# Four transformer-like layers on one NeuronCore: when a softmax loop sums its values, and what stands beside them

## The chip, the core and the metric

The kernel runs on one core of a Trainium2 chip. TensorE (PE) multiplies matrices, VectorE (DVE), ScalarE (ACT) and GpSimd (POOL) work on rows of 128 partitions, and SyncE (SP) issues most DMAs. The metric is the device time in microseconds from the first to the last instruction of one execution; the median of three executions is given, with the lowest and the highest.

## The reference, cut to what matters

`x` is 4 batches of 512 tokens with 288 features, all in fp32. Layer L0 rotates 64 of its directions per batch. L1, L2 and L3 are attention blocks with 16 heads of 18 features, each modulated by a condition; L1 and L2 end in an MLP of width 1152, L3 in a mixture of four experts, two per token. L2 also normalizes each query and each key head. The loop that changes computes this, for each of 12 attentions (3 layers by 4 batches):

```python
scores = jnp.einsum('blhd,bmhd->bhlm', q * scale, k)
attn = jax.nn.softmax(scores, axis=-1)
o = jnp.einsum('bhlm,bmhd->blhd', attn, v).reshape(b, l, c)
```

## The kernel before, in words

`attend(n, ...)` is called for attention n = 0 to 11, layer n // 4 and batch n % 4. Its 16 heads are taken in four groups of four, G = 4n to 4n + 3, because a head has 18 features and so fits in a strip of 32 partitions. A group has eight steps, so `attend` has 32. A step does two things with the scores of four heads, and both write a PSUM tile of 128 by 1024 of the same ring of two (`pbig`):

- `maxima` works ten steps ahead (`LOOK = 10`). Two matmuls give scores `p_s` with queries down the partitions, and DVE's `tensor_reduce` takes their maxima into `M`.
- `weigh` works at the step itself. Two matmuls give scores `p_st` with keys down the partitions, and ACT's exponential turns them into `e`, a ring of six.

Each of these matmuls has 32 rows and uses one of PE's four strips of rows, so the four of a step lie side by side. Before `weigh` may start on a group, `take_maxima` transposes its maxima (`p_m`, four transposes) and DVE subtracts them from the queries in place (`Q`, in `store`).

`give_values` sums the values: for one tile of 128 keys, four matmuls with 128 rows and 32 columns each (`p_av`), one per head, lie side by side in four strips of columns. A tile of keys takes two steps of `weigh`, so `ready` gets an entry at each odd step. After a group's fourth tile, ACT copies `p_av` to `o`, and five DMAs take it to DRAM.

What else PE has to do stands in generators that `attend` draws from, the `fill`: `project` makes queries, keys and values of attention n + 1 (`p_qk`, `p_v`), `finish` the output projection of attention n - 1 (`p_o`), `layernorm` the transposed input (`p_t`) of the next projection and the next MLP, and L2's `project` also the variances of its heads (`p_var`). Each `yield` names the piece's cost in us. `attend` adds a share of the attention's total to `left` after each step and draws pieces until `left` is used up: 0.5 us more at odd steps and 0.5 less at even ones, since even steps also sum values. The second generator, `norms`, draws one small DVE piece per step: statistics and normalized rows (`s`, `mv`, `rstd`, `xn`) and the inverse sums (`oc`). After attention 1 to 8, `mlp` runs the MLP of attention n - 1 in one stretch (`p_h`, `p_y`), with one call of `give_values` in its first part.

288 features are 128 + 128 + 32. `project` therefore works in pairs of jobs: the two full matmuls of each job, and then the tails, two matmuls with 32 rows that lie side by side in two strips. They come wherever `left` happens to run out.

Engines execute in the order in which the program issues, so the order of the Python calls is the order on each queue. A matmul in fp32 is two passes in the profile.

Of the kernel before, what the change touches and what calls it, by code (L numbers as in the profile page):

```python
# [17 lines left out]
NT = 4  # L18
# [5 lines left out]
NG = 4  # L24
# [23 lines left out]
def cond_seq_kernel(ctx: ExitStack, tc: tile.TileContext, a: dict, out: bass.AP):  # L48
# [227 lines left out]
    gtab = rows.tile([6 * B, C], F32, name="gtab")  # L276
    btab = rows.tile([2, B, C], F32, name="btab")

    md = mods.tile([128, C], F32, name="md")
    nc.gpsimd.memset(md, 0.0)  # L280
    was = {}

# [14 lines left out]
    def modulations(ns):  # L297

        for n in ns:
            l, half = divmod(n, 2)  # L300
            if half == 0:
                mt = mts[l] = const.tile([128, 4, KW + 1, B], F32, name=f"modT{l}")
                nc.gpsimd.memset(mt, 0.0)
            gr = mods.tile([B, C], F32, tag="gr", name=f"gr{n}")
            p = pmm(f"p_mod{n}")
            for k in range(KC):
                for s in range(3):
                    matmul(p[s * 32:s * 32 + B, :C], scT[0:kk(k), k, :],
                           was[n][0:kk(k), k, s * C:(s + 1) * C], start=(k == 0), stop=(k == KC - 1))
                yield 0.5  # L310
            for s in range(2):
                q = (2 * half + s) * 32
                scalar.copy(md[q:q + B], p[s * 32:s * 32 + B, :C])
            scalar.copy(gr, p[64:64 + B, :C])
            dma(gtab[n * B:(n + 1) * B], gr)
            if half and l < 2:
                br = mods.tile([B, C], F32, tag="br", name=f"br{l}")
                load(br, row(a[("L1_cond_b_fc2", "L2_cond_b2")[l]]).to_broadcast([B, C]))
                nc.gpsimd.tensor_mul(br, br, gr)
                dma(btab[l], br)  # L320
            if n == 5:
                sr = mods.tile([B, C], F32, tag="br", name="sr")
                scalar.activation(sr, p[32:32 + B, :C], AF.Copy, bias=1.0)
                dma(mrow.rearrange("s b c -> (s b) c")[0:B], md[64:64 + B])
                dma(mrow.rearrange("s b c -> (s b) c")[B:2 * B], sr)
                dma(mrow.rearrange("s b c -> (s b) c")[2 * B:], gr)
            if n + 2 < 6:
                load_ada(n + 2)
            if half:
                pt = pmm(f"p_modT{l}")  # L330
                for k in range(KW + 1):
                    w = 128 if k < KW else TAIL
                    transpose(pt[:w, k * 128:(k + 1) * 128], md[:, k * 128:k * 128 + w], ident)
                    for i in range(1 if k < KW else STRIPS):
                        scalar.copy(mts[l][i * TAIL:i * TAIL + w, :, k, :],
                                    pt[:w, k * 128:(k + 1) * 128].rearrange("p (s r) -> p s r", r=32)[:, :, :B])
                for s in (1, 3):
                    nc.gpsimd.tensor_scalar_add(mts[l][:, s], mts[l][:, s], 1.0)
                modT.append(mts[l])
                yield 0.6  # L340
# [20 lines left out]
    with tc.tile_pool(name="l0", bufs=1) as l0, tc.tile_pool(name="l0w", bufs=2) as l0w, \  # L361
# [4 lines left out]

        zP = hT[1][:, 0:2, :]
        MT = hT[1][0:D, KW, 0:B * D]
        At = mods.tile([D, C], F32, name="At")
        X = l0.tile([D, 2 * D], F32, name="X")  # L370
        Wt = l0.tile([D, D], F32, name="Wt")
        pt = pmm("p_G")
# [638 lines left out]
    with tc.tile_pool(name="attn", bufs=2) as at:  # L1011
# [14 lines left out]

        def project(n, norm):

            l, b = divmod(n, B)
            wqk, wv = WA[l][:2]  # L1030
            h = hT[0]
# [4 lines left out]
            def qk_job(m):  # L1036
                w = min(QP, QK - m * QP)
                cols = slice(m * QP, m * QP + w)
                p = pmm(f"p_qk{n}_{m}")

                def evict():
                    bias = QB[l][0:w, m:m + 1]
                    t = at.tile([QP, T], F32, tag="stage", name=f"stage{n}_{m}", bufs=3)[0:w]
                    if l != 1:
                        scalar.activation(t, p[0:w], AF.Identity, bias=bias, scale=scol[0:w, m:m + 1])
                    else:
                        tmp = at.tile([128, 2, T], F32, tag="e", name=f"tmp{n}_{m}", bufs=6)
                        sq, rs = tmp[0:w, 0, :], tmp[0:w, 1, :]
                        scalar.activation(sq, p[0:w], AF.Square, bias=bias)
                        vector.tensor_scalar(t, p[0:w], bias, None, ALU.add)  # L1050
                        yield 0.0
                        pv = pmm(f"p_var{n}_{m}")
                        matmul(pv[0:w], varsel.rearrange("p h d -> p (h d)")[0:w, 0:w], sq, start=True, stop=True)
                        scalar.activation(rs, pv[0:w], AF.Ln, bias=eps5[0:w])
                        scalar.activation(rs, rs, AF.Exp, scale=-0.5)
                        yield 0.86
                        vector.scalar_tensor_tensor(t, t, gains[0][0:w, m:m + 1], rs, ALU.mult, ALU.mult)
                        nc.gpsimd.tensor_scalar(t, t, gains[1][0:w, m:m + 1], None, ALU.add)
                    dma(flat[cols], t)
                return p[0:w], 0.86, lambda k, r: (wqk[r, k, cols], h[r, k, :]), evict  # L1060
# [12 lines left out]
            for i in range(0, len(jobs), 2):  # L1073
                pair = []
                for job, arg in jobs[i:i + 2]:
                    p, cost, operands, evict = job(arg)
                    for k in range(KW):
                        matmul(p, *operands(k, slice(0, 128)), start=(k == 0), stop=False)
                        yield cost
                    pair.append((p, operands, evict))  # L1080
                for e in later:
                    yield from e
                for q, (p, operands, evict) in enumerate(pair):
                    matmul(p, *operands(KW, strip(q)), start=False, stop=True)

                later = [e for e in [evict() for p, operands, evict in pair] if next(e, None) is not None]
                yield 0.95
                if i <= NQ - 1 < i + 2:
                    for e in later:
                        yield from e  # L1090
                    later = []

                    src = qd.rearrange("(s g i) d t -> s i d g t", s=2, i=4)
                    for s, t in enumerate((Q[n % 2], K[n % 2])):
                        for q in range(4):
                            dma(t[q * HS:q * HS + HD], src[s, q])
                    for q in range(4):
                        dma(Q[n % 2][q * HS + HD:q * HS + VS], zero_row[q:q + 1].rearrange("a (g t) -> a g t", t=T))
                    there.add(n)
                    yield None  # L1100
# [88 lines left out]

        def attend(n, fill, total, norms):  # L1190

            left = 0.0
            for step in range(8 * NG):
                g, s = divmod(step, 8)
                G = NG * n + g
                ahead, mstep = divmod(8 * G + s + LOOK, 8)
                if ahead < NG * NB:
                    while ahead // NG not in there:
                        next(fill)
                    maxima(ahead, mstep)  # L1200
                E.append(weigh(G, s))
                if s == 8 - 2 and G + 1 < NG * NB:
                    take_maxima(G + 1)
                if s % 2 == 0:
                    give_values()
                left += total / (8 * NG) + (0.5 if s % 2 else -0.5)
                next(norms, None)
                while left > 0:
                    cost = next(fill, "end")
                    if cost == "end":  # L1210
                        break
                    left -= cost or 0.0
                if s % 2:
                    ready.append((G, s // 2))
            for _ in fill:
                pass
            for _ in norms:
                pass

        def give_values():  # L1220

            if not ready:
                return
            G, c = ready.pop()
            if c == 0:
                PO[0] = pacc(f"p_av{G}")
            sum_values(G, PO[0], c, E[:2])
            del E[:2]
            if c == NT - 1:
                t = at.tile([128, T], F32, tag="o", name=f"o{G}", bufs=3)  # L1230
                scalar.copy(t, PO[0])
                n, g = divmod(G, NG)
# [61 lines left out]
        for t in range(LOOK):  # L1294
# [1 line left out]
            if t == 8:  # L1296
                take_maxima(0)
            next(rest, None)
            next(new)
            if t == 5:  # L1300
                projection_bias(0)
        for n in range(NB):
# [49 lines left out]
            if 2 <= n < 2 + 2 * NE:  # L1352
                fill_table(n - 2)
            attend(n, itertools.chain(*fill), total, first_ready(side))
            if n == 2 or n == B + 2:
                projection_bias(l + 1)
                head_biases(l + 1)
# [156 lines left out]
```

## Time and profile before

| what | us |
|---|---|
| median of 3 runs (lowest to highest) | 2094.88 (2086.53 to 2099.71) |
| profiled execution | 2086.44 |
| its span | 2084.7 |
| PE busy in the span | 1901.0 |
| DVE busy | 928.8 |
| ACT busy | 781.3 |
| the twelve attentions, from first to last score step (213.7 to 1647.4), the eight MLPs in between included | 1433.7 |
| one MLP with the step before it, mostly | 39.9 |
| the experts and what follows | 437.3 |

An attention starts at its first `weigh`: attention 1 at 300.6, attention 4 at 699.7, attention 8 at 1240.0 and so on. In the timeline a row is a run of instructions of one kind on one engine, with its start, its length, its shape (rows x columns of the stationary operand, or output and input), and in brackets the idle time of the engine before it, with what ended it. Most rows have L60 as their line, that of the helper (`InOrder`) through which the kernel calls PE, DVE and ACT, so rows are told apart by their tiles. In a table of stretches each engine's busy us stand with the number of instructions, and PEclk is the share of PE's full clock that was granted.

### The profile page before, as it was taken

The page shows a single profiled execution, that of the slowest core. Times are in us where ns is not written, and L with a number is a line of the kernel's source. Part 1 is how long each engine was busy: PE and PEld are TensorE (multiplying, and loading weights), DVE is VectorE, ACT ScalarE, POOL GpSimd, SP SyncE. Part 2 cuts the span into 40 slices and gives each one's busy share as a digit, 9 for nine tenths or more (in the row PEclk, how much of TensorE's full clock was granted, in tenths as well). Part 3 has the DMA queues.
Part 4 walks back from the last instruction along what each step waited for, and adds up shares of the span by engine and source line. Part 5 has one row for each costly group of instructions (what it writes and reads, how often), then busy time and mean ns, then how long its engine had stood idle before and what let it go on. Part 6 is the DMA issues. An engine that isn't in the chain of part 4 may idle for free. (4 is left out here: it accounts for less than half of the span.)

```text
span 2084.7 us, 26249 instructions
## 1 busy us (share of the span) xinstructions
PE 1901.0 (91%) x10269; PEld 927.7 (44%) x10269; DVE 928.8 (45%) x1953; ACT 781.3 (37%) x1169; POOL 252.2 (12%) x362
## 2 busy tenths in 40 slices
PE   6769879999999999899999999998987899999997
PEld 4544223343523434234234343333322367777775
DVE  6764646346164362562634526355576334111111
ACT  5122454434254343443444434444444322212111
POOL 1000010001010020010100000000000212332322
PEclk9578999999999999999999999999999989999999
DMA  3212152031131221511203112061221445766663
GB/s 97 71 40 62 37 153 81 17 96 29 40 73 26 72 58 42 135 42 54 75 22 85 33 54 80 23 137 30 82 50 61 172 147 175 238 187 219 203 202 95
DMA packets 89420, 187.23 MB, mean 90 GB/s; under 512 B 25454, under 2 KB 50457, under 8 KB 86803
## 3 DMA queue, kind: packets, MB, share of 16 engines
q1 hardware_dynamic: 77462, 103.39, 18.8%
q0 software_dynamic: 11248, 79.79, 11.8%
q10 hardware_dynamic: 584, 2.36, 0.4%
q8 instruction: 81, 1.33, 0.3%
q14 instruction: 45, 0.36, 0.1%
HBM read 152.49 MB, written 55.45 MB: 100 GB/s over the span
## 5 line engine op out<-in xcount | busy, mean ns | idle before, releaser
L60 DVE TENSOR_REDUCE store<-p_s 128x2 f32<-128x1024 f32 x384 | 470.4, 1225 | 370.3 <-PE p_st L60 324.0
L60 ACT ACTIVATE e<-p_st 128x1024 f32<-128x1024 f32 x384 | 393.1, 1024 | 643.9 <-PE p_st L60 639.6
L60 PE MATMUL p_s<-store 32*128 32x512 f32 x1536 | 445.4, 652 | 83.0 <-DVE store L60 81.7
L60 PE MATMUL p_st<-store 32*128 32x512 f32 x1536 | 444.2, 655 | 0.9 <-DVE store L60 0.9
L60 PEld LDWEIGHTS p_s<-store 32*128 32x128 f32 x1536 | 120.6, 186 | 315.9 <-DVE store L60 230.1
L60 PE MATMUL p_av<-e,store 128*32 128x512 f32 x1536 | 212.5, 626 | 2.0 <-ACT e L60 2.0
L60 PE MATMUL p_he<-hTe,store 128*128 128x256 f32 (+1 forms) x1026 | 200.1, 404 | 4.2 <-DVE hTe L60 4.2
L60 PE MATMUL p_ye<-store,hide 128*128 128x288 f32 x684 | 175.0, 415 | 7.2 <-ACT hide L60 7.2
L60 ACT ACTIVATE hide<-p_he,store 128x256 f32<-128x256 f32 x171 | 68.7, 472 | 281.7 <-PE p_he L60 281.7
L60 PEld LDWEIGHTS p_he<-hTe,store 128*128 128x128 f32 (+1 forms) x1026 | 147.7, 191 | 53.0 <-issue 30.5
L695 POOL TENSOR_TENSOR x<-x,gated 128x288 f32<-128x288 f32 x80 | 64.0, 800 | 837.0 <-DVE gated L60 837.0
L60 PE MATMUL p_qk<-hT,wqk 128*126 128x512 f32 (+1 forms) x360 | 162.3, 619 | 0.3 <-DVE store L60 0.3
L60 PE MATMUL p_h<-hT,w 128*128 128x512 f32 (+1 forms) x432 | 156.7, 618 | 5.2 <-DVE store L60 5.2
L60 PEld LDWEIGHTS p_ye<-store,hide 128*128 128x128 f32 x684 | 130.3, 193 | 46.9 <-ACT hide L60 11.0
L60 DVE TENSOR_TENSOR gated<-p_y,gate 128x288 f32<-128x288 f32 x32 | 14.7, 458 | 286.2 <-PE p_y L60 286.2
L60 PE MATMUL p_y<-w,hid 128*128 128x288 f32 x576 | 141.8, 407 | 0.0
L60 PEld LDWEIGHTS p_y<-w,hid 128*128 128x128 f32 x576 | 108.8, 190 | 35.5 <-issue 6.1
L60 PEld LDWEIGHTS p_st<-store 32*128 32x128 f32 x1536 | 118.0, 186 | 9.2 <-issue 6.2
L60 PEld LDWEIGHTS p_h<-hT,w 128*128 128x128 f32 (+1 forms) x432 | 60.7, 189 | 99.7 <-issue 83.6
L60 PE MATMUL p_o<-wp,oc 126*128 126x288 f32 (+1 forms) x288 | 94.6, 450 | 1.3 <-DVE oc L60 1.3
L60 DVE COPY hTe<-p_te 128x512 f32<-128x512 f32 x19 | 13.1, 690 | 172.9 <-PE p_tf L60 127.8
L60 PEld LDWEIGHTS p_qk<-hT,wqk 128*126 128x126 f32 (+1 forms) x360 | 46.9, 177 | 95.9 <-issue 94.3
(248 smaller groups left out, 1723.1 us busy)
## 6 DMA issues: line engine op xcount, KB each, us to landing
store<-qd SPq DMA_DIRECT2D x96, 144.0 KB
qd<-stage SPq DMA_DIRECT2D x48, 252.0 KB
od<-o SPq DMA_DIRECT2D x192, 36.0 KB
rd<-rd SPq DMA_DIRECT2D x12, 576.0 KB
oc<-od SPq DMA_DIRECT2D x24, 252.0 KB
rb<-rd SPq DMA_DIRECT2D x24, 252.0 KB
etab<-in_L_cond_w_dram SPq DMA_DIRECT2D x4, 1296.0 KB
etab<-in_L_cond_w_dram SPq DMA_DIRECT2D x8, 576.0 KB
```

The source lines that it names most:

```text
L60: ins = f(*args, **kw)
L695: nc.gpsimd.tensor_add(x[b][:, j, :], x[b][:, j, :], t)
```

## The change

Four things change in the loop.

1. `give_values` sums every tile that is ready in one run. `attend` calls it at steps 0 and 4 of a group, so two tiles of keys, eight matmuls, follow each other; no fill is drawn at such a step. The other six steps of a group get the fill, `total / (6 * NG)` each, without the half microsecond more or less.
2. `project` yields `"strips"` ahead of a pair's tails. `attend` then stops drawing, and the tails go right behind the scores of the next step, at any step, ahead of its values or its fill.
3. `take_maxima` moves from step 6 of a group to step 7, ahead of the fill.
4. L2's squares and inverse deviations (`sq`, `rs`) leave the ring of `e`. They share one tile, `spare`, in two halves, which also takes the place of four small tiles of the start (`md`, `gr`, `br`, `At`).

```diff
@@ project
-                        tmp = at.tile([128, 2, T], F32, tag="e", name=f"tmp{n}_{m}", bufs=6)
-                        sq, rs = tmp[0:w, 0, :], tmp[0:w, 1, :]
+                        sq = rs = spare[0:w, m % 2 * T:(m % 2 + 1) * T]
...
                 for e in later:
                     yield from e
+                yield "strips"
                 for q, (p, operands, evict) in enumerate(pair):
                     matmul(p, *operands(KW, strip(q)), start=False, stop=True)
@@ attend
-            left = 0.0
+            left, strips = 0.0, False
...
                 E.append(weigh(G, s))
-                if s == 8 - 2 and G + 1 < NG * NB:
-                    take_maxima(G + 1)
-                if s % 2 == 0:
+                if strips:
+                    left -= next(fill)
+                    strips = False
+                next(norms, None)
+                if s % 4 == 0 and ready:
                     give_values()
-                left += total / (8 * NG) + (0.5 if s % 2 else -0.5)
-                next(norms, None)
-                while left > 0:
-                    cost = next(fill, "end")
-                    if cost == "end":
-                        break
-                    left -= cost or 0.0
+                else:
+                    left += total / (6 * NG)
+                    if s == 8 - 1 and G + 1 < NG * NB:
+                        take_maxima(G + 1)
+                    while left > 0:
+                        cost = next(fill, "end")
+                        strips = cost == "strips"
+                        if cost == "end" or strips:
+                            break
+                        left -= cost or 0.0
@@ give_values
-            if not ready:
-                return
-            G, c = ready.pop()
-            if c == 0:
-                PO[0] = pacc(f"p_av{G}")
-            sum_values(G, PO[0], c, E[:2])
-            del E[:2]
-            if c == NT - 1:
+            while ready:
+                G, c = ready.pop(0)
+                if c == 0:
+                    PO[0] = pacc(f"p_av{G}")
+                sum_values(G, PO[0], c, E[:2])
+                del E[:2]
+                if c < NT - 1:
+                    continue
@@ main loop
             attend(n, itertools.chain(*fill), total, first_ready(side))
+            if n == 2:
+                give_values()
```

More of the change, by code (lines that the diff above doesn't have):

```diff
@@ L277, in cond_seq_kernel @@
     btab = rows.tile([2, B, C], F32, name="btab")
-    md = mods.tile([128, C], F32, name="md")
+    spare = mods.tile([128, 4 * C], F32, name="spare")
+    md = spare[:, 0:C]
     nc.gpsimd.memset(md, 0.0)
@@ L303, in modulations @@
                 nc.gpsimd.memset(mt, 0.0)
-            gr = mods.tile([B, C], F32, tag="gr", name=f"gr{n}")
+            gr = spare[0:B, C:2 * C]
             p = pmm(f"p_mod{n}")
@@ L316, in modulations @@
             if half and l < 2:
-                br = mods.tile([B, C], F32, tag="br", name=f"br{l}")
+                br = spare[0:B, 2 * C:3 * C]
                 load(br, row(a[("L1_cond_b_fc2", "L2_cond_b2")[l]]).to_broadcast([B, C]))
@@ L321, in modulations @@
             if n == 5:
-                sr = mods.tile([B, C], F32, tag="br", name="sr")
+                sr = spare[0:B, 2 * C:3 * C]
                 scalar.activation(sr, p[32:32 + B, :C], AF.Copy, bias=1.0)
@@ L368, in cond_seq_kernel @@
         MT = hT[1][0:D, KW, 0:B * D]
-        At = mods.tile([D, C], F32, name="At")
+        At = spare[0:D, 3 * C:]
         X = l0.tile([D, 2 * D], F32, name="X")
@@ L1298, in cond_seq_kernel @@
             next(rest, None)
-            next(new)
+            if next(new) == "strips":
+                next(new)
             if t == 5:
```

## The prediction, on record before the changed kernel ran

> **What bounds the kernel now.** I read the page first, then the timeline of attention 8, then stretches of 3.4 us around the places where PE's clock falls.
>
> ```profile
> span 2084.7 us, 26249 instructions
> PE 1901.0 (91%) x10269; PEld 927.7 (44%) x10269; DVE 928.8 (45%) x1953; ACT 781.3 (37%) x1169; POOL 252.2 (12%) x362
> ...
> L60 DVE TENSOR_REDUCE store<-p_s 128x2 f32<-128x1024 f32 x384 | 470.4, 1225 | 370.3 <-PE p_st L60 324.0
> ...
> L60 PE MATMUL p_s<-store 32*128 32x512 f32 x1536 | 445.4, 652 | 83.0 <-DVE store L60 81.7
> ```
>
> PE is the bound on average, but its largest idle time, 83.0 us ahead of `p_s`, is ended by DVE: the maxima of the step before have to leave the PSUM ring. What this means for one step shows in PE's timeline.
>
> ```profile
> 1281.74 0.59 PE L60 MATMUL p_st<-store 32*128 32x512 f32 x2
> 1282.17 0.59 PE L60 MATMUL p_qk<-hT,wqk 32*72 32x512 f32 x1
> ...
> 1282.60 0.59 PE L60 MATMUL p_qk<-hT,wqk 32*72 32x512 f32 x1
> 1283.12 1.92 PE L60 MATMUL p_o<-wp,oc 126*128 126x288 f32 x6
> ...
> 1286.04 1.06 PE L60 MATMUL p_av<-e,store 128*32 128x512 f32 x8
> 1287.42 0.70 PE L60 MATMUL p_s<-store 32*128 32x512 f32 x2 [0.32 <-DVE store L60]
> ```
>
> The same attention with all engines, around a step that has nothing beside its scores:
>
> ```profile
> 1299.63 0.70 PE L60 MATMUL p_s<-store 32*128 32x512 f32 x2
> ...
> 1300.80 1.23 DVE L60 TENSOR_REDUCE store<-p_s 128x2 f32<-128x1024 f32 x1 [0.61 <-PE p_st L60]
> ...
> 1302.08 0.77 PE L60 MATMUL p_s<-store 32*128 32x512 f32 x2 [1.31 <-DVE store L60]
> ...
> 1303.32 1.23 DVE L60 TENSOR_REDUCE store<-p_s 128x2 f32<-128x1024 f32 x1 [0.70 <-PE p_st L60]
> ...
> 1304.46 0.68 DVE L60 TENSOR_TENSOR store<-store,p_m 128x512 f32<-128x512 f32 x1
> ```
>
> Three things are to be seen. A pass of another shape starts 0.52 after the last one (1282.60 to 1283.12), one of the same shape 0.43 (1281.74 to 1282.17): a change of shape costs 0.09. A step with scores alone (1299.63 to 1302.08) lasts 2.45 although PE works for about 1.06 of it, since the maxima are ready 2.40 after its start. And a step with one tile of values (1286.04) also waits, 0.32. So 2.45 is the floor of every step; filling work is free up to there, and costs in full beyond.
>
> ```profile
> 361.60:365.00 3.40, 2.08 (x14) 0.87 (x18) 2.05 (x4) 1.02 (x1) 0.79 (x1) 1.00 0.27 76
> 365.00:368.40 3.40, 3.40 (x16) 0.99 (x15) 1.99 (x3) 1.42 (x3) 0.00 (x0) 0.50 0.00 0
> 870.20:873.60 3.40, 1.06 (x6) 0.18 (x2) 2.09 (x4) 0.17 (x1) 0.95 (x1) 1.00 0.60 205
> 873.60:877.00 3.40, 1.54 (x8) 0.52 (x8) 2.41 (x3) 0.00 (x0) 0.61 (x1) 0.50 0.23 76
> 1423.10:1426.50 3.40, 2.08 (x20) 0.47 (x16) 2.09 (x2) 1.77 (x2) 0.34 (x1) 1.00 0.00 0
> 1426.50:1429.90 3.40, 3.40 (x20) 1.69 (x17) 1.17 (x3) 0.57 (x2) 0.79 (x1) 1.00 0.00 0
> ```
>
> The columns after the length are PE, PEld, DVE, ACT, POOL busy, clock, DMA. After a stretch with 2.08 us of PE the clock was halved once (365.0) and once not; after 1.06 it was halved.
>
> **The change, part by part.** I took the order of the matmuls on PE in both programs and priced each of the first 31 steps of all attentions (372): scores 1.06, one tile of values 0.86 (two passes of 0.43), a full matmul 0.86 with 512 columns and 0.485 with 288, a transpose 0.11, a change of shape 0.09; a step counts at least 2.45. Before, this gives 937.7 of work and 83.1 of shortfall, 1020.8; the trace has 1099.7, the rest being half clock and the waits below. The sum of the change:
>
> 1. Changes of shape fall from 889 to 691: 198 x 0.093 = -18.4.
> 2. Nine tiles of values and eleven groups of `p_m` leave these steps: 9 x 0.86 + 11 x 0.44 = -12.5. The values come back, eight beside an MLP, which has no floor, one after attention 11: 9 x 0.86 = +7.8. The `p_m` there is hidden by the 0.86 idle ahead of `p_h`.
> 3. Shortfall. Before, 73 steps with values alone lack 0.35 each, and that disappears: a run of eight is 1.06 + 1.72 + 0.19 = 2.97. But the fill is thinner and breaks off at each "strips": steps with nothing beside the scores go from 16 to 59, and 43 x 1.39 = 59.8 is added. With the other thin steps the shortfall is 130.5: +47.4.
> 4. Maxima a step later. `weigh` of the next group needs the queries that DVE has reduced by `p_m`, and at step 7 that is the very next step. DVE does it in 0.68 once the step's own maxima are done (2.40), so `p_st` starts no sooner than 3.13; where the piece of `norms` queued ahead is `xn`, 3.56, the statistics, 3.77, the four small ones of `rstd` (0.19 each), 3.89; L2's `stage` and value copy, 4.34. `p_st` blocks everything queued behind it on PE, values and fill alike. Work in these steps is 1.7 to 4.3; step by step the excess over max(work, 2.45) adds up to 28. Before, step 7 covered it. Bounds: 12, if the small DVE pieces slip in ahead of the reduce, and 36.
> 5. Three groups of `p_t` now fall into one step. ACT takes them out in rows of 0.76 (four or five of them), 3 to 3.8 us ahead of the next exponential: 0.5 to 1 in each of eight attentions, +6 (0 to 10). Before has a like wait at steps 29 to 31, 0.45 in eight attentions: -4.
> 6. `finish` is earlier in attentions 1, 2, 7 and 8, so the MLP's `xn` are ready when `p_t` comes, where the trace has four waits of 1.0: -4 (-8 to 0).
> 7. L2. In the trace `stage` and value copies stand ahead of the reduce on DVE (749.38, 750.04, reduce at 750.41), because the tails ended the step before; with `p_var` waiting twice that is 3.1 in each of four attentions. Tails right behind scores put the reduce first: -12. Against it, `p_var` at step 7 takes the third PSUM buffer that `p_m` holds until DVE has subtracted: +0.9 x 4, and DVE is late once at step 14: +0.7 x 4. Together -6 (-12 to +4). That `sq` and `rs` leave the ring of `e` costs nothing by itself: at most five of six are held, and the halves of `spare` come free a pair later. The DMAs of `o` and `stage` keep their places on SP within a step or two; rows of `od` take 1.4, and their readers come five steps later.
> 8. Clock. PE's trace, cut into 3.41 us stretches as the clock changes lie, had half clock after 10 of 10 stretches with under half PE busy, 4 of 9 between 0.5 and 0.6, 2 of 13 up to 0.65. [...] After the change 28 pairs of thin steps follow each other, where before none did. Laid over the steps, that is about 14 halved stretches; before had 17 in the attentions, many from waits that go (617, 873, 1023). I take +5 (-10 to +20).
>
> Sum: -18.4 - 12.5 + 7.8 + 47.4 + 28 + 6 - 4 - 4 - 6 + 5 = +49. The profiled execution took 2086.44 (span 2084.7, 1.7 around it), so 2135.7; the median of the runs lies 8.4 higher, with runs on both sides, and I add half: 2140.
>
> **The rivals.** *Only the floor counts (chance 0.17).* DVE's subtraction slips in early (12 in place of 28), L2 gains its full 12, the clock gains 10: +49 - 16 - 6 - 15 = +12, about 2105. For it: the spare DVE time in every step (45% busy). Against: DVE is in order, and the maxima of step 7 are queued first.
>
> *Faster (0.05).* One mechanism: a run of eight values gives DVE and ACT 2.97 us, and if they then ran ahead, the bare steps behind it would not wait. The change breaks even when a bare step costs 2.45 - 49/59 = 1.6. At the 1.06 of PE's work it gains 59 x 1.39 = 82, giving 2058. Against it: scores wait for the maxima of the step directly before, and nothing can be stored up; nearly all the 16 bare steps of the trace last 2.45 to 2.55.
>
> *Half clock follows the bare steps (0.18).* The end of ten attentions (steps 29, 30) is bare and a full-speed MLP follows eight of them; if each begins with 1 or 2 halved stretches at 1.7 each, +15 to +27 over my +5: 2160.
>
> *The change doesn't do what it says:* in the new order the values do come in eights, but 17 of the runs have tails beside them, and fill is missing at many steps where it was meant to be. That is in the counts.
>
> **How the numbers follow.** Likeliest (0.60): 2140, by itself 2120 to 2155. With the floor case and the half clock case the range is 2104 to 2166, which leaves out the faster case and a few per cent at each end. A measurement can tell about 1% from no change, 2074 to 2116: faster 0.05; same 0.17, the floor case; slower 0.78.
>
> **What would show it.** Right: about 59 steps of 2.45 with scores alone; `p_st` in place of `p_s` waiting for DVE's store at the first step of a group, 20 to 30 us in all; runs of eight `p_av` with no wait behind them; `p_y` and the experts unchanged; attentions 0 and 10 some 7 us longer, 2, 7 and 8 some 3. Wrong: bare steps well under 2.45, or a subtraction that ends before step 7's reduce. It would also be wrong if the waits on DMA (`oc` at 871, 3.6 us) move from attention 5 to others, which I can't see in an order of instructions.

## The result, and the profile after

The changed kernel takes 2161.66 us (median of four runs, 2156.21 to 2167.67) against 2094.26 for the kernel before: a ratio of 1.0335, 95% interval 1.0292 to 1.0378. It is slower, as forecast, and the time lies in the forecast range, but 22 us above the likeliest value. The profiled execution took 2167.67, 81.2 more than the profiled execution before. The first lines are the page of the changed kernel: busy times, and the groups with their count, busy time, mean ns, and idle time before them with what ended it.

```profile
span 2166.0 us, 26245 instructions
...
PE 1948.6 (90%) x10269; PEld 956.6 (44%) x10269; DVE 930.3 (43%) x1953; ACT 782.7 (36%) x1169; POOL 252.0 (12%) x362
...
L60 DVE TENSOR_REDUCE store<-p_s 128x2 f32<-128x1024 f32 x384 | 470.4, 1225 | 460.5 <-PE p_st L60 400.7
...
L60 PE MATMUL p_s<-store 32*128 32x512 f32 x1536 | 460.4, 676 | 107.4 <-DVE store L60 104.1
```

Two things have grown. PE's idle time ahead of `p_s` went from 83.0 to 107.4: most of that is the floor, as predicted. But PE is also 47.6 us longer *busy* with the same 10269 matmuls, and its score matmuls last 676 ns on the mean where they lasted 652. Work that is the same and lasts longer is the clock: its mean is 0.936 in this execution and 0.957 in the profiled one before.

The steps themselves look as the prediction drew them. PE's timeline in attention 8, a run of eight, and a step with nothing beside its scores:

```profile
1300.42 1.92 PE L60 MATMUL p_av<-e,store 128*32 128x512 f32 x16
1302.28 0.70 PE L60 MATMUL p_s<-store 32*128 32x512 f32 x2
...
1304.73 0.70 PE L60 MATMUL p_s<-store 32*128 32x512 f32 x2 [1.31 <-DVE store L60]
```

The step with the run lasts from 1299.35 to 1302.28, 2.93 (2.92 from `p_st` to `p_st`, which is how steps are measured below), and `p_s` behind it does not wait. The bare step lasts 2.45 and its successor waits 1.31. The same attention, all engines, where the maxima are transposed at step 7:

```profile
1356.23 0.65 PE L60 MATMUL p_m<-ident,store 128*128 128x128 f32 x4
1356.29 1.23 DVE L60 TENSOR_REDUCE store<-p_s 128x2 f32<-128x1024 f32 x1 [0.62 <-PE p_st L60]
...
1357.43 0.42 DVE L60 TENSOR_SCALAR xn<-x,mv,rstd 128x288 f32<-128x288 f32 x1
...
1357.77 0.68 DVE L60 TENSOR_TENSOR store<-store,p_m 128x512 f32<-128x512 f32 x1
...
1358.60 0.70 PE L60 MATMUL p_st<-store 32*128 32x512 f32 x2
...
1358.61 0.76 PE L60 MATMUL p_v<-wv,hT 32*128 32x288 f32 x4
...
1359.65 1.92 PE L60 MATMUL p_av<-e,store 128*32 128x512 f32 x16
```

DVE takes the queued reduce, then `xn`, then the subtraction, and only then may `p_st` start, 3.43 after the step before it began. The tails (`p_v`) and the run of eight stand behind it. This too was drawn right.

What was not is in the table of 3.4 us stretches (columns after the length: PE, PEld, DVE, ACT, POOL busy, clock, DMA share, GB/s). First the end of attention 6 and the start of the MLP behind it, then attention 7's end, then two places in attention 10:

```profile
1102.20:1105.60 3.40, 2.81 (x12) 0.60 (x8) 2.17 (x2) 1.23 (x2) 0.00 (x0) 1.00 0.00 0
1105.60:1109.00 3.40, 3.28 (x11) 1.53 (x12) 1.22 (x2) 1.20 (x2) 0.00 (x0) 0.50 0.02 5
1109.00:1112.40 3.40, 3.40 (x9) 1.23 (x7) 0.76 (x2) 0.64 (x1) 0.00 (x0) 0.50 0.01 5
1112.40:1115.80 3.40, 3.40 (x12) 2.52 (x12) 1.08 (x4) 0.21 (x2) 0.00 (x0) 0.50 0.00 0
1115.80:1119.20 3.40, 3.40 (x5) 1.35 (x4) 1.00 (x3) 0.00 (x0) 0.00 (x0) 0.50 0.00 0
...
1242.10:1245.50 3.40, 1.14 (x8) 0.31 (x8) 2.17 (x2) 2.00 (x2) 0.00 (x0) 1.00 0.01 2
1245.50:1248.90 3.40, 3.13 (x12) 1.23 (x12) 1.22 (x2) 1.07 (x2) 0.00 (x0) 0.50 0.02 5
...
1586.90:1590.30 3.40, 1.64 (x11) 0.41 (x3) 3.14 (x6) 1.41 (x3) 2.42 (x4) 0.99 0.44 137
1590.30:1593.70 3.40, 2.77 (x13) 0.90 (x17) 0.24 (x1) 0.77 (x2) 0.58 (x1) 0.50 0.73 214
1593.70:1597.10 3.40, 3.40 (x20) 0.57 (x14) 1.54 (x5) 0.84 (x1) 0.00 (x0) 0.50 0.25 99
...
1624.40:1627.80 3.40, 2.72 (x12) 0.71 (x16) 3.04 (x8) 0.68 (x2) 0.00 (x0) 0.50 0.00 0
1627.80:1631.20 3.40, 3.40 (x20) 0.91 (x16) 0.63 (x1) 0.55 (x1) 0.00 (x0) 0.50 0.00 0
```

A thin stretch (1.14 us of PE at 1242.1, 1.64 at 1586.9) is followed by half clock, and what stands next then runs at half speed: the start of an MLP, or a run of eight values. (The fall behind 1102.2 has no thin stretch ahead of it, since PE was busy for 2.81 there.) PE's timeline of the step at 1591.3:

```profile
1591.33 1.22 PE L60 MATMUL p_s<-store 32*128 32x512 f32 x2
...
1593.35 3.64 PE L60 MATMUL p_av<-e,store 128*32 128x512 f32 x16
1596.93 0.76 PE L60 MATMUL p_s<-store 32*128 32x512 f32 x2
```

The run takes 3.64 in place of 1.92, and its step 5.59 in place of 2.92.

Split with the same priced order as in the prediction, the two profiled executions compare as follows ("steps" are the first 31 of each attention; "above the floor" is measured time less max(work, 2.45)):

| us | before | after | difference |
|---|---|---|---|
| floored sum of the steps | 1020.8 | 1037.2 | +16.4 |
| above the floor, steps at full clock | 46.1 | 52.3 | +6.2 |
| above the floor, steps touched by half clock | 32.7 | 66.7 | +34.0 |
| of these, steps with a run of eight (16 of 87 touched) | 0 | 32.9 | +32.9 |
| step 31 of attentions 1 to 8 with the MLP | 326.7 | 350.2 | +23.5 |
| time at half clock in those | 3.4 | 32.1 | +28.7, worth half: 14 |
| the other last steps | 7.4 | 11.5 | +4.1 |
| the experts and what follows | 437.3 | 434.3 | -3.0 |

### The profile page after: what moved, and what is told of

Its sections match the earlier page's. It is cut to its first block, busy times and chain, and to the rows that moved or that the text cites. A ratio compares the mean times of both kernels' runs of the same rounds, so it can differ in the third digit from the quotient of the medians.

```text
span 2166.0 us, 26245 instructions
## 1 busy us (share of the span) xinstructions
PE 1948.6 (90%) x10269; PEld 956.6 (44%) x10269; DVE 930.3 (43%) x1953; ACT 782.7 (36%) x1169; POOL 252.0 (12%) x362
## 5 line engine op out<-in xcount | busy, mean ns | idle before, releaser
L60 PE MATMUL p_s<-store 32*128 32x512 f32 x1536 | 460.4, 676 | 107.4 <-DVE store L60 104.1
L60 PE MATMUL p_st<-store 32*128 32x512 f32 x1536 | 459.4, 676 | 3.2 <-DVE store L60 2.0
L60 PE MATMUL p_av<-e,store 128*32 128x512 f32 x1536 | 204.1, 652 | 0.1
L60 PEld LDWEIGHTS p_he<-hTe,store 128*128 128x128 f32 (+1 forms) x1026 | 145.9, 189 | 52.3 <-issue 30.5
L60 PE MATMUL p_h<-hT,w 128*128 128x512 f32 (+1 forms) x432 | 162.1, 632 | 1.7 <-DVE store L60 1.7
L60 PEld LDWEIGHTS p_st<-store 32*128 32x128 f32 x1536 | 121.5, 192 | 28.3 <-issue 13.8
L60 PEld LDWEIGHTS p_av<-e,store 128*32 128x32 f32 x1536 | 42.3, 116 | 148.6 <-issue 146.9
```

The costliest lines, as they stand in the source:

```text
L60: ins = f(*args, **kw)
```

## The experiments

**How the runs are read.** Each execution has a span and a mean granted clock, and span x (1 - clock) is the PE time lost to half clock. Across the 98 executions of this study, of 13 kernels, the executions of one and the same kernel differ by 0.84 us of span for each us of lost clock (standard error 0.03), and are then 1.8 us (rms) from that line: run-to-run differences here are clock, and little else (the clock is recorded to 0.001, about 2 us of lost clock). So each kernel's difference can be split into a clock part (0.84 x the difference in lost clock) and a rest. For the changed kernel, over eight executions: span +71.1, lost clock 130.0 against 91.3, so +32.6 by the clock and +38.5 by the rest. All rows are held against the 34 executions of the kernel before together; against the seven that ran beside e1 to e4 alone, which lost 87.5, the clock parts of those four would be 3 higher, and the rests about the same. (The step with a run of eight at 1591.3, all at half clock, is 2.66 longer for 2.80 of lost clock, so weight 1 is the other end: +38.7 and +32.5.)

| kernel | ratio (95%) | lost clock | clock part | rest |
|---|---|---|---|---|
| before | 1 | 91.3 | 0 | 0 |
| changed | 1.0335 (1.0292 to 1.0378) | 130.0 | +32.6 | +38.5 |
| e1 maxima at step 6 again | 1.0309 (1.024 to 1.0379) | 130.9 | +33.4 | +25.8 |
| e2 no break ahead of the tails | 1.0318 (1.0269 to 1.0367) | 127.3 | +30.3 | +32.0 |
| e3 runs of eight alone | 1.0225 (1.0157 to 1.0294) | 128.0 | +31.0 | +16.4 |
| e4 extra work in bare steps | 1.0372 (1.033 to 1.0414) | 109.2 | +15.1 | +61.4 |
| e6 changed, old rhythm where fill is thin | 1.0252 (1.0192 to 1.0312) | 118.3 | +22.8 | +31.6 |
| e7 changed, extra work where fill is thin | 1.0468 (1.045 to 1.0485) | 121.3 | +25.3 | +75.3 |
| e8 before, the same extra work | 1.014 (1.0107 to 1.0174) | 101.3 | +8.5 | +27.1 |
| e9 runs of eight, not where fill is thin | 1.0107 (1.0048 to 1.0166) | 101.6 | +8.7 | +12.0 |
| e10 runs of eight where fill is thick | 1.0019 (0.999 to 1.0049) | 97.0 | +4.8 | -0.2 |
| e11 as e7, other operands | 1.0383 (1.0326 to 1.044) | 107.7 | +13.8 | +64.5 |
| e12 break alone | 1.0059 (1.0025 to 1.0093) | 83.2 | -6.8 | +17.0 |

The changed kernel run once more (e5) has a ratio of 1.0314 (1.0256 to 1.0373); its executions are in the second row's split. At first the theory was the prediction's, that floors and late maxima set the time, with the clock and the runs of eight themselves as rivals. After e1 to e3 it became that half clock does, where runs of eight leave thin steps behind; in e9 to e12 this is theory A. Each expectation says what its letters stand for.

### The parts undone: e1, e2, e3

e1 takes the maxima back to step 6:

```diff
                     left += total / (6 * NG)
-                    if s == 8 - 1 and G + 1 < NG * NB:
+                    if s == 8 - 2 and G + 1 < NG * NB:
                         take_maxima(G + 1)
```

> The changed kernel with the transposed maxima back at step 6, ahead of the fill. Theory A (floor of 2.45 us per step, late maxima, and half clock after thin steps): the waits of p_st at the first step of a group, 27 us by the order of instructions, go, floor and shape changes stay (53 bare steps, 1036.1 us of floored steps against 1037.2): 2162 - 27 = 2135, down to 2120 if half clock shrinks with the waits. Theory B (the run of eight values is what costs: it delays exponentials and their readers): 2155 to 2165.

e2 takes out the break; the tails go where `left` runs out, as before:

```diff
                     yield from e
-                yield "strips"
                 for q, (p, operands, evict) in enumerate(pair):
```

> The changed kernel without the break ahead of the tails, which come where the fill runs out, as before. Theory A: bare steps fall from 59 to 40, floored steps from 1037.2 to 1015.3 us, the wait for late maxima from 27 to 22: 2162 - 27 = 2135, less 0 to 15 of clock. Theory B: 2155 to 2165, and up to 11 more if the tails' place behind the scores was worth their changes of shape (718 instead of 691) on top of that.

e3 has both edits, so that of the loop's changes only the runs of eight and the fill at six of eight steps are left.

> The changed kernel with both undone, so that the values in runs of two key tiles and the even shares of the fill are left (and the squares outside of the exponentials' ring). Theory A: floored steps 1014.4 us against 1020.8 before, 7.8 more beside the MLPs, no wait for late maxima, L2's waits as before: 2094 + 1, and 0 to 20 for half clock after 27 pairs of thin steps, so 2095 to 2115. Theory B: most of the loss stays, 2140 to 2160.

Measured: 2147.37, 2150.03 and 2135.4 against 2084.0. Each part undone gains less than expected. The distances to the kernel before, 63, 66 and 51, are those of theory B (61 to 71 for e1, 61 to 82 for e2, 46 to 66 for e3) and not of theory A (26 to 41, 26 to 41, 1 to 21): the runs of eight are what costs. Theory B's reason, late exponentials and readers, is another matter. The runs alone, at which the floors see next to nothing (1014.4 and 7.8 beside MLPs, together +1.4), already cost 2.25%. The split says why. They bring the whole clock part, +31.0 of +32.6; the break and the late maxima add none that can be told from the spread of four executions. (No kernel here has the runs without the fill at six of eight steps, so the two are not told apart.) In e3's trace 14 of the 87 runs of eight are touched by half clock and stand 31.5 above the floor. In the rest, the late maxima cost 12.7 (changed less e1) to 15.6 (e2 less e3), and the break on top of runs of eight 6.5 (changed less e2) to 9.4 (e1 less e3).

### The price of a bare step: e12

```diff
@@ project, in the kernel before
+                yield "strips"
                 for q, (p, operands, evict) in enumerate(pair):
@@ attend
+                if strips:
+                    left -= next(fill)
+                    strips = False
...
-                    if cost == "end":
+                    strips = cost == "strips"
+                    if cost == "end" or strips:
                         break
```

> The kernel before with the break ahead of the tails alone: the drawing of fill stops there, and the tails go right behind the next scores; values every two steps, maxima at step 6. Bare steps go from 16 to 40, but none of them stands next to another thin one (pairs of thin steps 0). By the floors 1050.2 against 1020.8, +29.4; the prediction's gain in L2 (DVE's stage and value copies no longer ahead of the maxima) is 12 at most. Theory A (floors price it, and single thin steps do not cost clock): +17 to +29 us, ratio 1.008 to 1.014. If single bare steps cost clock as well: above 1.018. If the work that fails to fit below the floor is made up later: below 1.005.

Measured: 2096.86 against 2089.02, ratio 1.0059, a little under theory A's lower end of 1.008. The rest is +17.0, and +29.4 - 12 is 17.4: the floors price the break. Bare steps rose from 16 to 40 and the lost clock *fell*, from 91.3 to 83.2. So bare steps that stand singly add no half clock here; that part of the rival is refuted. The time above the floor at full clock fell from 46.1 to 35.7 in its trace.

### Where the clock is lost: e9 and e10

e9 is e3 with the order of before in the three attentions whose fill is thin; e10 keeps it in the last group of every attention as well.

```diff
@@ attend, against e3
+            sparse = n in (0, NB - 2, NB - 1)
...
-                if s % 4 == 0 and ready:
+                if s == 8 - 2 and G + 1 < NG * NB:
+                    take_maxima(G + 1)
+                summed = s % (2 if sparse else 4) == 0 and bool(ready)
+                if summed:
                     give_values()
-                else:
-                    left += total / (6 * NG)
...
+                if sparse or not summed:
+                    left += total / (8 * NG) + (0.5 if s % 2 else -0.5) if sparse else total / (6 * NG)
```

(In e10 `sparse` holds for `g == NG - 1` too, and the last share is `total / (6.5 * NG)`.)

> The kernel with the runs of eight alone (maxima at step 6, no break ahead of the tails), but attentions 0, 10 and 11, which have little filling work, keep the order of before: one tile of values every two steps, fill at each step. By the floors of the prediction its scored steps sum to 1009.9, before's to 1020.8, and seven tiles of values (+6.0) go beside an MLP: -4.9 us. Theory A (a run of eight is only dear where it leaves thin steps behind it, because PE's clock is then halved and the runs themselves are paid at half clock; pairs of thin steps fall from 27 to 9): between before's time and +18 us over it, ratio 1.000 to 1.009. Rival B (a run of eight costs something wherever it stands, and the clock is a bystander): 9 of 12 attentions keep their runs, so three quarters of the 2.25% of the runs alone: ratio 1.017.

> As the kernel before it in this list, and the last group of every attention, where the filling work runs out, keeps the order of before too; the fill's share is total / (6.5 * NG) at the steps that draw. No two thin steps follow each other any more (0 pairs, before 0), 16 bare steps as before, 800 changes of shape (before 889), all values inside the scored steps. By the floors 1006.8 against 1020.8. Theory A: -14 us, ratio 0.993 (0.988 to 0.999). Rival B (a run itself costs): 27 of 48 groups have runs, 0.56 of 2.25%: ratio 1.013. If the floors hold and the clock does not care, also 0.993, so this run tells A from B but not A from a bystander clock.

Measured: 2109.85 and 2090.61 against 2089.02, ratios 1.0107 and 1.0019. Both lie between the two theories, and the split separates them. Keeping the runs of eight out of 3 of 12 attentions takes 22 of e3's 31 us of clock part away; keeping them out of the thin groups too leaves 4.8. Rival B, three quarters of the loss in e9 and 0.56 of it in e10, fits neither. So the clock is lost where thin steps and runs of eight meet, not by runs of eight as such. (No kernel here has pairs of thin steps without runs, so what the pairs alone would do is not shown.) The rest of e9 falls by 4.4 from e3's, where the floors and the values beside MLPs fall by 6.3. But against the kernel before all three stand too high: e3's rest is +16.4 where the floors and the values beside MLPs gave +1.4, e9's +12.0 where they gave -4.9, e10's -0.2 where they gave -14. These 14 to 17 us have one kind of place. e10, all engines and SP's queue, attention 5:

```profile
878.21 1.01 ACT L60 ACTIVATE e<-p_st 128x1024 f32<-128x1024 f32 x1
879.99 1.19 SPq L1158 DMA_DIRECT2D rb<-rd  x3
881.28 0.57 SPq L1246 DMA_DIRECT2D sd<-o  x1
881.89 1.54 SPq L1248 DMA_DIRECT2D od<-o  x4
883.53 0.82 SPq L1061 DMA_DIRECT2D qd<-stage  x2
886.12 0.75 DVE L60 TENSOR_SCALAR stage<-p_qk,qkb 126x512 f32<-126x512 f32 x1 [7.93 <-DMA qd<-stage]
886.78 1.22 DVE L60 TENSOR_REDUCE store<-p_s 128x2 f32<-128x1024 f32 x1
...
888.05 1.22 PE L60 MATMUL p_s<-store 32*128 32x512 f32 x2 [10.20 <-DVE store L60]
```

DVE wants to fill `stage` again, which the transfer to `qd` must have left first; SP issues that transfer only at 883.53, behind the inverse sums' `rb` and the five transfers of `o`. The maxima are queued behind it on DVE, and PE waits 10.20. The kernel before waits 4.21 at this place, mostly for `rb` (3.56), e3 9.81, e9 9.77, e2 6.54, the changed kernel 3.64, e1 2.04.

Attentions 3, 4 and 6 also prepare L2's queries and keys, and have like waits. PE's waits of over 1.4 us in the steps of attentions 3 to 6 sum to 10.9 in the kernel before, 25.7 in e3, 25.9 in e9, 23.9 in e10, 9.9 in the changed kernel and 8.7 in e1; e12 has none. In e3, e9 and e10 the longest one of each attention follows a wait of DVE for the transfer to `qd` (2.25 to 9.29); in the kernel before, DVE nowhere waits over 0.7 for it. Beside them e3 and e9 have four of 1.66 ahead of `p_var`, ended by DVE's subtraction. So these waits are 13 to 15 of the 14 to 17 us, as far as one trace of each kernel shows. The first kind is the wait on DMA that the prediction named as one it could not see in an order of instructions. It also makes the break cheap on top of runs of eight: the floors charge 21.7 for it (1036.1 in e1 against 1014.4 in e3), and the waits are 17.0 shorter with it, which leaves some 5 where 9.4 was measured.

### The same place in the changed kernel: e5 and e6

e5 is the changed kernel once more; e6 has e9's `sparse` attentions in the changed kernel, with its break and its late maxima.

> The changed kernel once more, on the chip of the three others of this batch. Both theories: 1.029 to 1.038 of before. It is the base that the two next runs are held against.

> The changed kernel, but attentions 0, 10 and 11, whose fill is modulations and routes with little matmul work, sum their values every two steps and draw fill at each step, as before. Theory A2 (values in long runs leave thin steps in front of them, PE's clock halves there, and the run itself is then paid at half clock): floored steps 1030.4 against 1037.2, and the half clock of these three attentions falls from about 85 to under 45 us: 25 to 35 us below the changed kernel. Theory B2 (the loss is in the dense attentions, by late maxima and breaks, and the clock is a bystander): 5 to 10 us below it.

Measured: 2151.67 and 2142.15 against 2089.86. The difference of 9.5 is B2's number (5 to 10), and not A2's (25 to 35). In the profiles attention 10 falls from 123.4 (e5) to 100.8, attention 0 from 93.4 to 86.6, but attention 11 rises from 88.8 to 103.8: there the clock stayed halved for eleven stretches in a row. The rest falls by 6.9, just the floors' 6.8 (1030.4 against 1037.2); the clock part only by 9.8, where the same edit gained 22 from e3 to e9. Why it gains less with the break and the late maxima in place is open.

### Filling the thin steps: e4, e7, e8, e11

e4 adds a matmul of 128 x 512, whose result is not read, to steps that draw no fill; e7 to the thin stretches of attentions 0, 10 and 11 of the changed kernel; e8 does the like to the kernel before.

```diff
@@ attend, e7 (e4: if drawn == 0.0 and not was_strips)
+                if s % 4 and step >= {0: 9, NB - 2: 17, NB - 1: 0}.get(n, 99):
+                    busy_work(G, s)
...
+        def busy_work(G, s):
+
+            p = pmm(f"p_idle{G}_{s}")
+            matmul(p, ident, Q[0][:, 0, :], start=True, stop=True)
```

> The changed kernel with one more matmul (128 rows, 512 columns, result unused) in each step that draws no fill and has no tails: bare steps fall from 59 to 11, and 54 us of PE work are added. Theory A: below the floor of 2.45 us this work is free, and half clock in the attentions, some 170 us of the profiled execution, falls to under 110: 2162 - 20 to - 35, so 2127 to 2142. If the clock is not set by thin steps: 2155 to 2165. If the bare steps were not bound by the floor: up to 2205.

> The changed kernel with one more matmul (128 rows, 512 columns, result unused) at the end of each step without values in the thin stretches: attention 0 from step 9, attention 10 from step 17, all of attention 11. Floored steps rise by 12.9 us. Theory A2: runs of eight values in attention 10 fall from 5.6 to about 2.9 us, half clock in these attentions from 85 to under 40 us, and the time falls by 5 to 20 us against the changed kernel although PE does 49 us more. Theory B2: 10 to 15 us above the changed kernel.

> The kernel before with the same matmul at the odd steps of the same stretches. Floored steps rise by 10.2 us. Theory A2: before has 30 us of half clock in these attentions, so at most 15 us can be won back: between -5 and +8 us of before. Theory B2: +10 us.

Measured: e4 2164.33 against 2084.0, 80 more, which lies between the second (61 to 71) and the third (up to 111) of its cases; e7 2188.55 and e8 2123.43 against 2089.86. e7 and e8 contain a wait of their own making. The table of waits of e7, over attention 11 and what follows, names it (who waited for what: us in total, times, longest):

```profile
PE p_idle L60 <- DMA store<-etab,widx: 16.6, 1, 16.6
```

The extra matmul reads `store`, into which the experts' tables are being gathered there. e8 has the same wait with 13.6. So the time of neither says anything of the clock. e11 repeats e7 with the identity matrix as both operands:

```diff
+            for i in range(4):
+                matmul(p[:, i * 128:(i + 1) * 128], ident, ident, start=True, stop=True)
```

> The changed kernel with extra matmuls, whose result nobody reads, in the thin stretches of attentions 0, 10 and 11: four of 128 columns on the identity matrix, which no transfer writes, so that the wait of 16.6 us for the gathered tables, which the earlier form met in attention 11, cannot come. By the floors +13.3 us over the changed kernel. Theory A (half clock is what the thin stretches cost): the value runs of attention 10 at 2.92 in place of 5.59, attentions 0 and 10 lose 25 to 30 us of half clock against the profile of the changed kernel, the work adds 13: ratio 1.024 (1.020 to 1.030). Rival B (half clock is a bystander, the floors alone count): changed kernel + 13: ratio 1.039.

Measured: 2166.63 against 2089.02, ratio 1.0383: by the time, the rival's number (1.039), and not theory A's 1.024. The trace gives theory A one half. At step 24 of attention 10, for one, PE's timeline of e11 reads

```profile
1604.31 1.13 PE L60 MATMUL p_s<-store 32*128 32x512 f32 x4
...
1605.93 1.92 PE L60 MATMUL p_av<-e,store 128*32 128x512 f32 x16
```

so the run takes 1.92 and its step 2.92, where the changed kernel had 5.59. Half clock in the steps is 64.4 us, where the two profiles of the changed kernel have 130.6 and 106.8 (e5), and over the four executions the clock part from +32.6 to +13.8. But the extra matmuls add 26.0 to the rest where the floors gave 13.3, and e4's 22.9: the gain is eaten. That added PE work brings the clock back is shown; as a remedy it is worth nothing.

Why it costs more than its floor shows in part in single steps, at full clock in both traces. In e4 eleven of the matmuls stand at step 31, eight of them directly ahead of an MLP, where there is no floor (attention 3: 41.20 to 42.65, but attention 8: 41.20 in both), and four at step 7 or 23 behind a late `p_st`, where each adds about 1.0 (step 23 of attention 2: 3.43 to 4.41). In e11 several stand in attention 11's last ten steps, which compute no maxima, so that 2.45 does not bind there (step 25: 2.90 to 3.99, step 29: 0.53 to 2.15). And half clock in bare steps, which the matmuls remove first, is worth less than in a run: a bare step wholly at half clock takes 3.40, 0.95 over the floor, and a run of eight 5.59, 2.66 over its 2.93. The whole is not accounted for.

Of these kernels none is faster than the one before; e10 comes within what can be told from it.

## Why the prediction was right, and where it was wrong

The sign and the range held, the range in part by luck: the likeliest case by itself ended at 2155, and the part above it came from a rival whose cause was wrong. The sum had two errors of opposite sign, of which the clock was by far the larger: the terms other than the clock came to +44 and measure +38.5 (or +32.5, by the other weight), and the clock, predicted +5, measures +32.6 (or +38.7).

- **Terms 1 to 3, the order of instructions.** Right. They came to -18.4 - 12.5 + 7.8 + 47.4 = +24.3, that is, the floored +16.4 and the values beside MLPs. Of the 59 bare steps the 48 at full clock have a median of 2.45; a run of eight, priced 2.97, takes 2.93. The run that tests it is e12: +17.0 measured for a floored +29.4 less term 7's 12.
- **Term 4, the late maxima.** The mechanism was right and the size was not: +28 predicted, 12.7 to 15.6 measured. The steps with `p_m` do stand 28.4 above the floor at full clock, about what was worked out, and 36.5 with the halved ones. But "before, step 7 covered it" was wrong: before, and in e1, the steps with `p_m`, halved ones included, stand 19.9 and 19.3 above the floor as well, some 17 less than 36.5, and I had counted an excess as a difference.
- **Terms 5 and 6**, +2 and -4, were not tried apart; they are inside the few us that the rest leaves over.
- **Term 7, L2.** The step with `p_var` at step 7 was priced with a wait of 0.9 and takes 4.77, 1.37 above its floor. The gain of 12 that the tails behind scores bring fits e12, where the waits of over 1.4 us in attentions 3 to 6, 10.9 before, are gone. What the term did not have is that with runs of eight the transfer of `stage` comes late, which the break happens to hide.
- **Term 8, the clock. This is the step that failed**: +5 (-10 to +20) predicted, outside its own bounds. The counts that it rests on held: after stretches with under half of PE busy the clock was halved 14 of 14 times in the changed kernel's trace too (counted from 27 us, where the clock's record begins), and between 0.5 and 0.6 10 of 20. My use of them did not. I said "about 14 halved stretches; before had 17 in the attentions, many from waits that go". The 31 first steps now have 130.6 us of half clock (38 stretches; 106.8 us in e5's trace of the same kernel) against 61.4 (18), and the waits stayed. I had counted how often the clock falls, not how long it stays down, and not what stands in the stretches that follow: a bare step at half clock goes from 2.45 to 3.40, a step with a run of eight from 2.93 to 5.59. The change puts just such a run behind thin steps: eleven of the 16 halved runs stand in attentions 0, 10 and 11 or at the first step of attention 1. (Three others, at step 16 of attentions 3, 5 and 6, stand behind a long wait and not behind bare steps.)
- **The rival "half clock follows the bare steps"** gave 2160, and its amount is what came. Its place is half right: four of eight MLPs begin at half clock (before: none; one has it further inside, before as after), and half clock beside MLPs is worth 14 more than before; the larger part sits in the runs of eight inside the attentions, 32.9 in the profile. Its cause in one word, bare steps, is wrong by e12, where 40 of them stand singly and the lost clock is 83.2 (before 91.3); in the changed kernel, with 130.0, 28 of the 59 stand next to another.
- **Attentions 2, 7 and 8** were to be some 3 longer, and are 2.6, 1.1 and 2.7. **Attentions 0 and 10** were to be some 7 longer, and are 11.8 and 25.4: there the fill is thin, four runs of attention 10 took 5.59, and the price had no clock in it.
- **The floor case** (2105) fell with the clock, and **the faster case** with the bare steps of 2.45. The experts and what follows changed by -3.0 us; they were to stay as they were, and lost 3.6 us less to half clock in this execution.

Neither a bare step nor the length of its gap decides by itself. In the stretch at 1242.1 shown above, the longest gap is 1.31, and it is followed by half clock; in the kernel before, the stretch from 1300.3 to 1303.7 has a gap of 1.31 too (ahead of 1302.08), and the clock stays at 1.00 behind it. e12's single bare steps cost no clock (83.2 us lost against 91.3 before). In these traces the fall goes with PE's share of a whole 3.41 us stretch more than with the longest gap inside it. Over the fourteen traces half clock followed 160 of 166 stretches at full clock with under half of PE busy, 87 of 180 between 0.5 and 0.6, 40 of 413 between 0.6 and 0.7, and 64 of 6953 above. Where the longest gap was under 1 us but the share under 0.6, it followed 42 of 49; where the gap was over 1 us but the share between 0.6 and 0.7, 23 of 337. The share does not explain all: why the clock falls behind 1102.2 is open.

## What to carry to other kernels

Where steps have a floor set by another engine, as here (2.45 us, by DVE's maxima), spreading PE's work evenly can be worth more than fewer changes of shape (198 fewer were worth 18.4 us, by the prices of the prediction, and none of these kernels became faster): it fills the floor, and it leaves fewer 3.4 us stretches so thin that half clock follows (the steps before have 18 halved ones, the changed ones 38). When a change gathers work into runs, ask what is left between the runs, and price the run itself at half clock where two thin steps stand ahead of it (here 5.59 in place of 2.93). Look at the order of the transfers as well: with the runs of eight one came late on its queue, and DVE waited for it (7.93 us in e10, attention 5). And an excess over a floor is a cost of the change only less the excess that the same steps had before.

## What the hardware showed that I had not expected

- In the changed kernel's trace the clock, once halved, came back only after a stretch in which PE was nearly always busy. Of its 81 halved stretches 31 ended in full clock: 29 of the 42 that were wholly busy, 2 of the 10 between 0.90 and that, and none of the 29 below 0.90. In the trace of the kernel before it came back once after less, 2.85 of 3.41 us at 1655.2.
- Being wholly busy was not enough either. From 1105.6 to 1119.2 PE was busy 3.28 to 3.40 of 3.40 us in four stretches, and the clock stayed at half; e3 has ten such in a row in attention 11, e6 eleven, e8 thirteen. What ends them the traces do not show.
- The executions of one kernel differ by their clock almost alone: the kernel before ranges from 2073.9 (0.962) to 2096.0 us (0.952) of span on one chip, and span x clock is 1995.1 and 1995.4; in the 19 executions there it lies between 1988.8 and 1996.3, a third of the range of the spans.
